# Group-norm statistics on ScalarE instead of VectorE, and more output buffers for the last image, in a fused attention and convolution kernel

## The chip, the cores and the metric

The kernel runs on one core of a Trainium2 chip. The core has a matrix engine (PE, TensorE; its weight loads are the rows PEld), a vector engine (DVE), an activation engine (ACT, ScalarE), a general engine (POOL, GpSimd) and a queue that only issues transfers (SP). ACT and SP both issue DMA transfers here. Every engine takes its instructions in order; an instruction that waits holds up all that stand behind it on the same engine. The metric is the device time of one execution in microseconds; smaller is better.

## The reference

Input x has the shape 16 x 56 x 56 x 384 (16 images of 3136 pixels, 384 channels), float32. Two layers are applied, each on a group-normalised copy of its input and added back to that input:

```python
def _gn(v, G=32, eps=1e-5):                 # per image and group of 12 channels
    g = v.reshape(B_, H_, W_, G, C_ // G)
    m = jnp.mean(g, axis=(1, 2, 4), keepdims=True)
    s = jnp.var(g, axis=(1, 2, 4), keepdims=True)
    return ((g - m) / jnp.sqrt(s + eps)).reshape(v.shape)
...
x = x + _L0_conv_ref(_gn(x), L0_conv_w_qkv, L0_conv_w_proj, L0_conv_b_proj)
x = x + _L1_conv_ref(_gn(x), L1_conv_w)
```

Layer 0 is a dilated attention: q, k and v are projections of the normalised x. The 384 channels are three groups of 128 with dilations 1, 2 and 3, each of four heads of 32 channels. Every pixel attends to its 3 x 3 dilated neighbours within its head: nine products of q and k, a softmax over the nine, and the weighted sum of nine v. The result is projected by w_proj and b_proj is added. Layer 1 is a 3 x 3 convolution, each channel by itself, with weights that are the signs of L1_conv_w.

The mean and the variance in `_gn` are what the change is about. They are over a whole image, so nothing of a layer can be normalised before all of that image's input to the layer is there.

## The kernel before

**Chunks and stages.** An image is cut into 7 chunks of 8 rows (448 pixels, PX), 112 chunks in all. On chip the channels are the partitions: a chunk is three tiles (j = 0, 1, 2) of 128 channels by 448 pixels. Three stages each run over all chunks, and work for different chunks is interleaved:

- *Stage A* (`plan_a`) loads x, turns it so that channels are partitions (PE, L412), copies the result from PSUM to `xa` on ACT (L424), takes its statistics on DVE (L425, `bn_stats`: count, mean and squared deviations of the even and of the odd elements, 6 numbers) and stores it to the DRAM scratch `xd`. Image 0 is kept in SBUF as `x_first` as well, and its store to `xd` is issued on ACT (L429); its 21 turns are all done ahead of any other work, because the first normalisation needs them all.
- *Stage B* (`plan_b`) normalises `xn` on ACT (L459), projects k and v (`pkv`) and q (`pq`) on PE (L463), copies k and v to SBUF on ACT (L473), forms the products `t` on DVE (L516), sums them over channels on PE (`ps`, L501), computes the softmax on ACT, DVE and POOL (`sT` L533, `ew`, `e`), spreads the weights over channels on PE (`pb_a`, L582), multiplies them with v on DVE (`w`, L589) and adds up on POOL (`w` L597, `y` L600 and L601). `out_project` multiplies y with w_proj on PE (`po`, L615), and DVE adds the bias and the residual (`xr`, L618) and takes the statistics of the new x (L621). The chunk is stored to the scratch `x1d`.
- *Stage C* (`plan_c`) loads from `x1d`, normalises on ACT (`z` L713, `zg` L756), convolves two channel groups on PE (`pc`, L727) and the third with ACT and POOL (`m`, L778 and L784), adds the residual (L734), turns the result back on PE (`pt_o`, L799), copies it to `osb` on ACT (L801) and stores it to the output (L804).

**Statistics.** At an image's last chunk `group_norm` combines them: `bn_aggr` on DVE over the 7 chunks of each j (L305, tile `ch`), sums over groups on PE (`pm`, `pb`, `pv`), the inverse root on DVE and POOL (`var`, L334 to L349), and the spread back to channels (`pp`, L354, to `mr`, L358, and for the convolution `mrz`, L372).

**The last image.** It is the tail: no later image covers it. Its stage C uses tiles that earlier stages have left (`z_last`, `xg_last`), DVE instead of POOL for the third channel group (L769), and issues its output on ACT. `osb` comes from pool `o_p` with two buffers: the third copy waits until the first one's transfer to the output has landed. The tiles `y`, in pool `y_p` with four buffers, are not used any more by then.

**What sets the order.** `at(when, order, piece)` gives each piece of work a time slot; a chunk takes 9 slots (STEP). Pieces are emitted by slot and, in a slot, by kind (SOFTMAX, SCORE, STATISTICS and so on). A scheduler then orders each engine's queue from this and adds the waits. Tiles of one tag share that tag's buffers in turn. In particular all PSUM tiles of tag `mt` (`pt_x`, `pkv`, `po`, `pc`, `pt_o` and those of the statistics) share three buffers, so PE's next such tile waits for an engine to have read the one three before it.

Of the kernel before, what the change touches and what calls it, by code (L numbers as in the profile page):

```python
# [8 lines left out]
F32 = mybir.dt.float32  # L9
BF16 = mybir.dt.bfloat16  # L10
I32 = mybir.dt.int32
AF = mybir.ActivationFunctionType
ALU = mybir.AluOpType
# [4 lines left out]
P = 128  # L18
HEADS = 4
HD = 32  # L20
NG = 3
# [3 lines left out]
SUB = 112  # L25
# [10 lines left out]
def dilated_attention_then_binary_conv(  # L36
# [28 lines left out]
    nc = tc.nc  # L65
    B, H, W, C = x.shape
    PX = ROWS * W
    NCH = H // ROWS
# [63 lines left out]
    bias = const.tile([P, NG], F32, name="bias")  # L132
# [12 lines left out]
    st_p = ctx.enter_context(tc.tile_pool(name="st_p", bufs=2))  # L145
# [5 lines left out]
    y_p = ctx.enter_context(tc.tile_pool(name="y_p", bufs=4))  # L151
# [5 lines left out]
    o_p = ctx.enter_context(tc.tile_pool(name="o_p", bufs=2))  # L157
# [137 lines left out]
    def group_norm(stats, done, for_convolution=False):  # L295
# [78 lines left out]

        return channels, mean, deviation, variance, invert, spread_out

    def chunk_of(dram, c):
        return dram.rearrange("(j p) n -> p j n", p=P)[:, :, c * PX : (c + 1) * PX]

# [2 lines left out]
    def at(when, order, piece):  # L382

        pieces.setdefault((when, order), []).append(piece)

    stats0, stats1 = {}, {}
# [4 lines left out]
    def plan_a(m, t0):  # L391

        b, c = divmod(m, NCH)
        had = {}

        def load():
            if c == 0:
                stats0[b] = st_p.tile([P, NG, NCH, 6], F32, tag="stats0", name="stats0")
                xd[b] = dr_p.tile([C, H * W], F32, tag="xd", name="xd")
            if b == 0 and c % 3:  # L400

                xin = z_p.tile([P, NQ * PX], F32, tag="z", name="xin_z")[:SUB, : NSUB * C]
                xin = xin.rearrange("p (s c) -> p s c", s=NSUB)
            else:
                xin = xin_p.tile([SUB, NSUB, C], F32, tag="xin", name="xin")
            had["xin"] = xin
            nc.sync.dma_start(xin, xf[b, c * PX : (c + 1) * PX, :].rearrange("(s p) c -> p s c", p=SUB))

        def turn(j):
            pt = ps_mt.tile([P, 512], F32, tag="mt", name="pt_x")  # L410
            for s in range(NSUB):
                nc.tensor.transpose(  # L412
                    pt[:, s * SUB : (s + 1) * SUB], had["xin"][:, s, j * P : (j + 1) * P], ident[:SUB, :SUB]
                )
            if b == 0:

                if j == 0:
                    pool, tag = ((xn_p, "xn"), (xn_p, "xn"), (xn_p, "xn"), (xr_p, "xr"), (t_p, "t"), (w_p, "w"),
                                 (w_p, "w"))[c]
                    first[c] = pool.tile([P, NG, PX], F32, tag=tag, name="x_first")  # L420
                xa = first[c][:, j]
            else:
                xa = xa_p.tile([P, PX], F32, tag="xa", name="xa")
            nc.scalar.copy(xa, pt[:, :PX])  # L424
            nc.vector.bn_stats(stats0[b][:, j, c, :], xa)  # L425
            if b:
                nc.sync.dma_start(xd[b][j * P : (j + 1) * P, c * PX : (c + 1) * PX], xa)
            elif j == NG - 1:
                nc.scalar.dma_start(chunk_of(xd[b], c), first[c])  # L429

        steps = {}

        def norm(k):
            if k == 0:
                steps["of"] = group_norm(stats0.pop(b), lambda mr: mr0.update({b: mr}))
            steps["of"][k]()

        at(t0 - 3 if b else FIRST + 2 * max(c - 2, 0), LOADS, load)
        for j in range(NG):
            at(t0 + 2 * j if b else FIRST + 2 * c + 1, STAGE_A, lambda j=j: turn(j))  # L440
        if c == NCH - 1:
            for k in range(6):
                at(t0 + 5 + STAT0_SLICE[k], STAT_ORDER[k], lambda k=k: norm(k))

    def plan_b(m, t0):

        b, c = divmod(m, NCH)
        had = {}

        def load_x():  # L450
            if m < 3:
                had["xn"] = first[m]
                return
            had["xn"] = xn = xn_p.tile([P, NG, PX], F32, tag="xn", name="xn")
            nc.sync.dma_start(xn, chunk_of(xd[b], c))
# [147 lines left out]
        def load_residual():  # L603
            had["xr"] = xr = xr_p.tile([P, NG, PX], F32, tag="xr", name="xr")
            nc.sync.dma_start(xr, chunk_of(xd[b], c))

        def out_project(j):

            if c == 0 and j == 0:
                stats1[b] = st_p.tile([P, NG, NCH, 6], F32, tag="stats1", name="stats1")  # L610
                x1d[b] = dr_p.tile([C, H * W], F32, tag="x1d", name="x1d")
            xr = had["xr"]
            po = ps_mt.tile([P, 512], F32, tag="mt", name="po")
            for g in range(NG):
                nc.tensor.matmul(  # L615
                    po[:, :PX], wprojT[:, g, j * P : (j + 1) * P], had[f"y{g}"], start=(g == 0), stop=(g == NG - 1)
                )
            nc.vector.scalar_tensor_tensor(  # L618
                xr[:, j, :], po[:, :PX], bias[:, j : j + 1], xr[:, j, :], op0=ALU.add, op1=ALU.add
            )  # L620
            nc.vector.bn_stats(stats1[b][:, j, c, :], xr[:, j, :])  # L621
            if j == NG - 1:
                nc.sync.dma_start(chunk_of(x1d[b], c), xr)

# [24 lines left out]
        for j in range(NG):  # L649
            at(t0 + 24 + j, PROJECT, lambda j=j: out_project(j))  # L650
# [4 lines left out]
    def plan_c(m, t0):  # L655

        b, c = divmod(m, NCH)
# [136 lines left out]
        def turn(s):  # L794
            pt = ps_mt.tile([P, 512], F32, tag="mt", name="pt_o")
            mid = had["xg"][:, 1 : ROWS + 1, :].rearrange("p r w -> p (r w)")
            for j in range(NG):
                src = mid if j == JG else had["x1"][:, j]
                nc.tensor.transpose(pt[:SUB, j * P : (j + 1) * P], src[:, s * SUB : (s + 1) * SUB], ident)  # L799
            osb = o_p.tile([SUB, C], F32, tag="osb", name="osb")  # L800
            nc.scalar.copy(osb, pt[:SUB, :C])  # L801

            queue = nc.sync if b < B - 1 else nc.scalar
            queue.dma_start(of[b, p0 + s * SUB : p0 + (s + 1) * SUB, :], osb)  # L804

        if b == B - 1:

            at(t0 - 12, LOADS, load_g)
            at(t0 - 3, LOADS, load_x)
            ahead = 8 if c else 1  # L810
            at(t0 - ahead, NORM, normalise_g)
            for j in range(JG):
                at(t0 - 12 + j, LOADS, lambda j=j: load(j))
                at(t0 - ahead + j, NORM, lambda j=j: normalise(j))
                at(t0 + 1 + j, CONVOLVE, lambda j=j: convolve(j))
            for ky in range(3):
                at(t0 + 1 + ky, CONVOLVE, lambda ky=ky: taps_last(ky))
            for s in range(NSUB):
                at(t0 + 12, STAGE_C, lambda s=s: turn(s))
            return  # L820
# [13 lines left out]
        for s in range(NSUB):  # L834
            at(t0 + 9 + s, STAGE_C, lambda s=s: turn(s))
# [51 lines left out]
```

## Time and profile before

| what | value |
|---|---|
| median of 8 runs | 5409.84 us (5406.19 to 5414.89) |
| the profiled execution, its own time | 5411.89 us |
| its span, first to last instruction | 5410.2 us |
| granted TensorE clock, mean | 0.981 |
| ACT L424, 128x448 copy of pt_x | 533 ns, x315 |
| ACT L459, normalise with two pointer operands, 128x448 | 751 ns, x327 |
| ACT L778, scale with one pointer operand, 128x448 | 658 ns, x945 |
| ACT L801, copy to osb, 112x384 | 481 ns, x448 |
| DVE L618, bias and residual | 678 ns, x336 |
| DVE L305, bn_aggr over 42 numbers | 336 ns, x96 |
| POOL L597, sum of weighted v, 128x1344 | 3051 ns, x672 |

A row of the profile's groups reads: line, engine, operation, output<-input, shapes, count | busy us, mean ns of one | idle us of the engine just ahead of them, and what ended that idle time. In a timeline a row is start, length, engine, line, operation and, in brackets, the idle time before it with its releaser. In the slices each digit is the busy share of a fortieth of the span in tenths. The list of waits gives the sum in us, how often, and the longest. The chain of waits is the work that ended last, followed back from the end.

### The profile page before, as it was taken

The page shows a single profiled execution, that of the slowest core. Times are in us where ns is not written, and L with a number is a line of the kernel's source. Part 1 is how long each engine was busy: PE and PEld are TensorE (multiplying, and loading weights), DVE is VectorE, ACT ScalarE, POOL GpSimd, SP SyncE. Part 2 cuts the span into 40 slices and gives each one's busy share as a digit, 9 for nine tenths or more (in the row PEclk, how much of TensorE's full clock was granted, in tenths as well). Part 3 has the DMA queues.
Part 4 walks back from the last instruction along what each step waited for, and adds up shares of the span by engine and source line. Part 5 has one row for each costly group of instructions (what it writes and reads, how often), then busy time and mean ns, then how long its engine had stood idle before and what let it go on. Part 6 is the DMA issues. An engine that isn't in the chain of part 4 may idle for free.

```text
span 5410.2 us, 77297 instructions
## 1 busy us (share of the span) xinstructions
PE 5202.6 (96%) x27669; PEld 2412.6 (45%) x27669; DVE 4153.8 (77%) x4209; ACT 2396.1 (44%) x4189; POOL 4215.2 (78%) x3049
## 2 busy tenths in 40 slices
PE   8999999999999999999999999999999999999965
PEld 4444444444444444444444444444444444444422
DVE  4887777878777787777878777787777877777753
ACT  3224444444444444444445444444444444444433
POOL 2677888878888887888878888888888888887880
PEclk9999999999999999999999999999999999999976
DMA  5444555655555555555655556555555555544443
GB/s 167 127 120 125 160 156 156 163 153 161 156 155 165 164 156 161 156 155 159 164 156 161 157 153 165 164 155 164 158 157 157 162 152 161 165 130 130 122 131 125
DMA packets 810799, 825.73 MB, mean 153 GB/s; under 512 B 359467, under 2 KB 800174, under 8 KB 810414
## 3 DMA queue, kind: packets, MB, share of 16 engines
q1 hardware_dynamic: 802430, 808.79, 53.9%
q10 hardware_dynamic: 7984, 12.00, 0.7%
q8 instruction: 219, 3.59, 0.3%
q14 instruction: 166, 1.36, 0.1%
HBM read 466.41 MB, written 231.21 MB: 129 GB/s over the span
## 4 chain that ended last, share of the span: by engine, by line
PE 72%; POOL 10%; DVE 6%; DMA 5%; ACT 4%; issue 2%; SPq 1%; POOLq 0%; ACTq 0%; DVEq 0%
PE pkv L463 22%; PE pq L463 12%; PE po L615 10%; PE ps L501 9%; PE pc L727 8%; PE pb_a L582 4%; POOL w L597 3%; POOL m L784 3%; DVE t L516 2%; PE pt_o L799 2%; PE pt_x L412 2%; DVE w L589 2%; ACT m L778 2%; DMA xg<-x1d 1%; POOL m L789 1%
## 5 line engine op out<-in xcount | busy, mean ns | idle before, releaser
L597 POOL TENSOR_TENSOR w<-w 128x1344 f32<-128x1344 f32 x672 | 2050.0, 3051 | 452.6 <-DVE w L589 388.7
L589 DVE TENSOR_TENSOR w<-pb_a,v 128x1344 f32<-128x1344 f32 x1008 | 1560.1, 1548 | 268.1 <-PE pb_a L582 177.9
L516 DVE TENSOR_TENSOR t<-pq,k 128x1344 f32<-128x1344 f32 x1008 | 1536.6, 1551 | 236.9 <-PE pq L463 235.9
L463 PE MATMUL pkv<-xn,wqkvT 128*128 128x448 f32 x3924 | 1568.4, 548 | 9.0 <-ACT xa L424 4.7
L463 PEld LDWEIGHTS pkv<-xn,wqkvT 128*128 128x128 f32 x3924 | 717.9, 190 | 671.7 <-issue 631.4
L615 PE MATMUL po<-y,wprojT 128*128 128x448 f32 x2016 | 838.4, 552 | 33.7 <-ACT k L473 15.8
L784 POOL TENSOR_TENSOR m<-m 128x1344 f32<-128x1344 f32 x210 | 644.7, 3070 | 282.5 <-ACT m L778 282.4
L463 PE MATMUL pq<-xn,wqkvT 128*128 128x448 f32 x1962 | 830.7, 557 | 0.0
L713 ACT ACTIVATE z<-z,mrz 96x448 f32<-96x448 f32 x840 | 578.2, 751 | 359.7 <-DMA z<-x1d 339.6
L501 PE MATMUL ps<-t,sel 128*32 128x448 f32 x6048 | 663.7, 548 | 27.8 <-DVE t L516 27.1
L778 ACT ACTIVATE m<-zg,ktap 128x448 f32<-128x448 f32 x945 | 555.5, 658 | 275.4 <-POOL m L784 268.3
L615 PEld LDWEIGHTS po<-y,wprojT 128*128 128x128 f32 x2016 | 377.6, 192 | 390.5 <-issue 342.3
L727 PE MATMUL pc<-z,kdiag 96*32 96x440 f32 (+1 forms) x5040 | 514.6, 541 | 6.6 <-POOL z L715 4.6
L463 PEld LDWEIGHTS pq<-xn,wqkvT 128*128 128x128 f32 x1962 | 343.9, 189 | 316.9 <-issue 316.9
L618 DVE SCALAR_TENSOR_TENSOR xr<-po,bias,xr 128x448 f32<-128x448 f32 x336 | 227.7, 678 | 230.6 <-PE po L615 226.9
L734 DVE TENSOR_TENSOR x<-pc,x 128x448 f32<-128x448 f32 x224 | 139.4, 623 | 344.3 <-PE pc L727 333.4
L582 PE MATMUL pb_a<-aT,spread 24*128 24x448 bf16 x3024 | 368.8, 359 | 32.3 <-DVE w L589 25.4
L601 POOL TENSOR_TENSOR y<-y,w 128x448 f32<-128x448 f32 x336 | 381.6, 1136 | 22.6
L600 POOL TENSOR_TENSOR y<-w 128x448 f32<-128x448 f32 x336 | 382.4, 1138 | 14.7
L473 ACT COPY v<-pkv 128x448 f32<-128x448 f32 x336 | 178.4, 531 | 480.7 <-PE pkv L463 472.4
L473 ACT COPY k<-pkv 128x448 f32<-128x448 f32 x336 | 178.2, 530 | 375.7 <-PE pkv L463 375.7
L501 PEld LDWEIGHTS ps<-t,sel 128*32 128x32 f32 x6048 | 170.2, 109 | 368.5 <-issue 252.3
(131 smaller groups left out, 4395.7 us busy)
## 6 DMA issues: line engine op xcount, KB each, us to landing
z<-x1d SPq DMA_DIRECT2D x570, 224.0 KB
xr<-xd SPq DMA_DIRECT2D x112, 672.0 KB
x1d<-xr SPq DMA_DIRECT2D x112, 672.0 KB
xn<-xd SPq DMA_DIRECT2D x109, 672.0 KB
xin<-in_x_dram SPq DMA_DIRECT2D x108, 672.0 KB
xd<-xa SPq DMA_DIRECT2D x315, 224.0 KB
out_dram<-osb SPq DMA_DIRECT2D x420, 168.0 KB
x<-x1d SPq DMA_DIRECT2D x112, 448.0 KB
```

The lines of the kernel that those rows point to most:

```text
L463: nc.tensor.matmul(dst[:, :PX], wqkvT[:, cc, o0 : o0 + P], had["xn"][:, cc, :], start=(cc == 0), stop=(cc == NG - 1))
L501: return nc.tensor.matmul(had["ps"][32 * j : 32 * j + 32, :PX], sel[:, s0 : s0 + 32], tk, start=(issued[j] == 1), stop=(issued[j] == len(r ...
L516: nc.vector.tensor_tensor(t.rearrange("p k (r w) -> p k r w", w=W), q3, k3, ALU.mult)
L582: return nc.tensor.matmul(pb[:, kx, :PX].rearrange("p (s n) -> p s n", s=NSUB), spread[rows_of, v % 2, :], had["a"][rows_of, :, v // 8, :] ...
L589: nc.vector.tensor_tensor(w.rearrange("p k (r w) -> p k r w", w=W), pb[:, :, :PX].rearrange("p k (r w) -> p k r w", w=W), three(kv[1][g][m ...
L597: nc.gpsimd.tensor_tensor(w0, w0, w, ALU.add)
L600: nc.gpsimd.tensor_tensor(y, w0[:, 0], w0[:, 1], ALU.add)
L615: nc.tensor.matmul(po[:, :PX], wprojT[:, g, j * P : (j + 1) * P], had[f"y{g}"], start=(g == 0), stop=(g == NG - 1))
L713: nc.scalar.activation(z, z, AF.Identity, bias=mrz[:, j, q, 0:1], scale=mrz[:, j, q, 1:2])
L727: return nc.tensor.matmul(pcr[q * HD : (q + 1) * HD, :, lo:hi], kdiag[:, kx, j * NQ + q, :], rows(set_of(j, q))[:, :, lo + kx - 1 : hi + k ...
L778: nc.scalar.activation(rows(t[:, kx]), zp[:, ky : ky + ROWS, kx : kx + W], AF.Copy, scale=ktap[:, o : o + 1])
L784: nc.gpsimd.tensor_tensor(had["m"], had["m"], t, ALU.add)
```

## The change

Two parts are changed.

*Statistics.* Where DVE had one `bn_stats` per tile there are now: a sum over the 448 pixels that the instruction writing the tile gives as a second output (`accum_out`: ACT's copy in `turn`, DVE's addition in `out_project`), a `mul` on ACT of 128x1 that makes the mean of it, and a `Square` on ACT over the whole tile, with the mean as bias, whose summed output is the squared deviation (its elementwise output goes to a tile `squares` of one buffer that nobody reads). An entry is now count, mean and squared deviation, 3 numbers, with the count set on POOL once per tile of statistics. `total`, the sum, has two buffers, shared by both layers. `bn_aggr` is as before, over 21 numbers.

*Output.* For the last image, `osb` is taken from the four buffers of `y` instead of the two of `osb`.

```diff
+    def new_statistics(name):
+
+        stats = st_p.tile([P, NG, NCH, 3], F32, tag=name, name=name)
+        nc.gpsimd.memset(stats[:, :, :, 0:1], float(PX))
+        return stats
+
+    def statistics(entry, xa, total):
+        nc.scalar.mul(entry[:, 1:2], total, 1.0 / PX)
+        squares = st_p.tile([P, PX], BF16, tag="squares", name="squares", bufs=1)
+        nc.scalar.activation(
+            squares, xa, AF.Square, bias=entry[:, 1:2], scale=-1.0, accum_out=entry[:, 2:3]
+        )
...
-            nc.scalar.copy(xa, pt[:, :PX])
-            nc.vector.bn_stats(stats0[b][:, j, c, :], xa)
+            total = st_p.tile([P, 1], F32, tag="total", name="total")
+            nc.scalar.activation(xa, pt[:, :PX], AF.Copy, accum_out=total)
+            statistics(stats0[b][:, j, c, :], xa, total)
...
+            total = st_p.tile([P, 1], F32, tag="total", name="total")
             nc.vector.scalar_tensor_tensor(
-                xr[:, j, :], po[:, :PX], bias[:, j : j + 1], xr[:, j, :], op0=ALU.add, op1=ALU.add
+                xr[:, j, :], po[:, :PX], bias[:, j : j + 1], xr[:, j, :], op0=ALU.add, op1=ALU.add, accum_out=total
             )
-            nc.vector.bn_stats(stats1[b][:, j, c, :], xr[:, j, :])
+            statistics(stats1[b][:, j, c, :], xr[:, j, :], total)
...
-            osb = o_p.tile([SUB, C], F32, tag="osb", name="osb")
+            if b < B - 1:
+                osb = o_p.tile([SUB, C], F32, tag="osb", name="osb")
+            else:
+                osb = y_p.tile([P, PX], F32, tag="y", name="osb_last")[:SUB, :C]
             nc.scalar.copy(osb, pt[:SUB, :C])
```

In the two places where a tile of statistics is made, `new_statistics` takes the place of a tile of 6 numbers per entry.

More of the change, by code (lines that the diff above doesn't have):

```diff
@@ L397, in load @@
             if c == 0:
-                stats0[b] = st_p.tile([P, NG, NCH, 6], F32, tag="stats0", name="stats0")
+                stats0[b] = new_statistics("stats0")
                 xd[b] = dr_p.tile([C, H * W], F32, tag="xd", name="xd")
@@ L609, in out_project @@
             if c == 0 and j == 0:
-                stats1[b] = st_p.tile([P, NG, NCH, 6], F32, tag="stats1", name="stats1")
+                stats1[b] = new_statistics("stats1")
                 x1d[b] = dr_p.tile([C, H * W], F32, tag="x1d", name="x1d")
```

## The prediction

> **What bounds the kernel now.** First the page's busy shares and slices.
>
> ```profile
> PE 5202.6 (96%) x27669; PEld 2412.6 (45%) x27669; DVE 4153.8 (77%) x4209; ACT 2396.1 (44%) x4189; POOL 4215.2 (78%) x3049
> PE   8999999999999999999999999999999999999965
> ```
>
> PE is full except in the first and the last two slices. The table by windows says how full (columns: window, its length, busy time and count for PE, PEld, DVE, ACT, POOL, granted clock, DMA share, GB/s).
>
> ```profile
> 1000.00:2000.00 1000.00, 987.14 (x5303) 459.79 (x5305) 789.39 (x793) 467.69 (x820) 820.32 (x566) 0.99 0.57 158
> 5250.00:5300.00 50.00, 34.20 (x246) 14.90 (x246) 19.89 (x43) 18.81 (x30) 6.94 (x24) 0.65 0.41 131
> ```
>
> In the middle PE idles 13 us in 1000, and its timeline inside an image runs from matmul to matmul without a gap. A freer VectorE can return at most what PE waits for there. The list of waits of PE between 100 and 5150 us (us in total, times, longest):
>
> ```profile
> PE ps L501 <- DVE t L516: 24.3, 35, 1.5
> PE po L615 <- ACT k L473: 15.8, 13, 2.7
> PE pb_a L582 <- DVE w L589: 11.0, 18, 1.0
> PE pv L331 <- POOL dev L325: 9.6, 11, 0.9
> ```
>
> So 35 us name DVE. DVE's timeline ahead of one such wait (PE idle 1.46 us until 1162.70) shows who was late: POOL, by 1.96 us, not bn_stats.
>
> ```profile
> 1158.79 1.56 DVE L589 TENSOR_TENSOR w<-pb_a,v 128x1344 f32<-128x1344 f32 x1 [1.96 <-POOL w L597]
> 1160.27 0.92 DVE L547 TENSOR_REDUCE sm<-ew 112x48 f32<-112x432 f32 x1
> 1161.09 1.56 DVE L516 TENSOR_TENSOR t<-pq,k 128x1344 f32<-128x1344 f32 x1
> ```
>
> What moves the end is therefore the two ends. At the start, PE's projections wait for image 0's statistics; at the tail, ACT's copies to osb wait for output transfers. Both chains are below.
>
> **What the Trainium skill says.** "ScalarE: Activation LUTs", section "What ACT_TABLE_LOAD costs": an ACTIVATE with immediates takes 186 ns + 0.833 ns per element, each pointer operand adds 93 ns, neighbours overlap by about 93 ns. The trace agrees: one pointer at 448 elements gives 652, measured 658 (m, L778); two give 745, measured 751 (xn, L459); three copies back to back took 1.40 us, a pitch of 0.435 for rows of 0.533. The page says that an ACTIVATE can give an accumulator output, but no price. "VectorE: DVE Perf Modes", section "Two Vector instructions with no wait between them": on VectorE such an op is two instructions, the second reading the accumulator; no row of before shows one. [...] The built program accordingly has mul wait for the sum and Square for mul, so these cannot overlap fully.
>
> **The change part by part.**
>
> ```profile
> L621 DVE BATCH_NORM_STATS2 stats<-xr 128x6 f32<-128x448 f32 x336 | 208.4, 620 | 3.8
> L425 DVE BATCH_NORM_STATS2 stats<-xa 128x6 f32<-128x448 f32 x315 | 191.3, 608 | 63.7 <-ACT xa L424 63.5
> ```
>
> *DVE loses* 208.4 + 191.3 + 11.9 (image 0) = 412 us, 3.7 us per chunk (46 us: the same wait of PE recurs after one image, 322.9 us, of 7 chunks), and bn_aggr reads 21 numbers instead of 42 (all 96 cost 31.9 us now). The sum added to L618 costs 0 to 0.13 us (DVE's smallest rows), at most 44 us. All beside PE. Of the 35 us I credit 3, since POOL sets the waits; bounds 0 and 35.
>
> *ACT gains* 672 mul of 128x1 (0.187 by the skill: 126 us), 672 Square with a bias pointer (0.658 as L778: 442 us) and 1008 sums. A sum's unknown cost lies between 0 (read in the shadow of the next instruction) and 0.19 (one more instruction of fixed cost); below nothing is excluded, since the copy itself stays. I take 0.1: 101 us. ACT goes from 2396 to 3065 us, 57%, or from 21.4 to 27.4 us per chunk. Three new couplings: mul waits for DVE's L618; L618 waits, through the two buffers of total, for an earlier mul; and bn_aggr on DVE waits for Square, with w and t queued behind it. Inside an image each has cover. Between k's copy (ends 681.5) and z (685.42, waiting 3.91 us for DMA) ACT is idle, which takes two mul and one Square. The other Square delays sT from 687.25 to about 688.1, and PE wants it at 690.52. If that cover went, it would cost up to 0.85 us per chunk. At the two statistics per image, bn_aggr can wait for a Square that stands behind a z waiting for DMA: I put 0.2 us for each of 15 images, +3 us, bounds 0 and 30.
>
> *32 memsets on POOL* (0.15 us, as L752) are 5 us in 1195 us of POOL idle time: nothing; uncovered, 5 us.
>
> *The start.* ACT's timeline:
>
> ```profile
> 8.13 0.53 ACT L424 COPY x_first<-pt_x 128x448 f32<-128x448 f32 x1 [3.54 <-PE pt_x L412]
> 16.64 1.40 ACT L424 COPY x_first<-pt_x 128x448 f32<-128x448 f32 x3 [3.17 <-DMA small<-in_L_conv_b_proj_dram]
> 36.14 1.04 ACT L424 COPY x_first<-pt_x 128x448 f32<-128x448 f32 x2
> ```
>
> The last bn_aggr ends at 41.56 us; ACT's copies are done at 37.2. Now all 21 statistics run on ACT. One chunk is 3 copies, 3 mul, 3 Square and the issue of xd: 1.45 (pitch 0.435, one overlap lost to a wait) + 0.53 + 1.78 (pitch 0.56, the last 0.66) + 0.41 = 4.2 us, 4.7 with sums at 0.1, 5.4 with 0.19. In the built order chunk 0's last Square and all of chunk 1 stand behind the xd issue, which waits for a small transfer as at 16.23 (now the next one of the queue, so about 17). From there: 0.7 + 6 x 4.7 + 9 weight copies (1.3 for three) 3.9 = 49.8, and 0.3 for bn_aggr: 50.1 against 41.56, +8.5. Next image's mul and Square between the first normalisations add 0.5. **+9**, bounds +5 (sums free) and +13. Nothing covers it: from 60 us on PE is full, so its work shifts whole.
>
> *The tail.* The chain of waits (start, us, what):
>
> ```profile
> 5366.44 5.87 DMA out_dram<-osb
> 5372.39 0.49 ACT osb L801
> ...
> 5378.14 3.26 DMA out_dram<-osb
> ...
> 5383.37 3.61 DMA out_dram<-osb
> ...
> 5396.19 3.85 DMA out_dram<-osb
> ...
> 5401.55 2.14 DMA out_dram<-osb
> ...
> 5404.27 2.09 DMA out_dram<-osb
> ```
>
> With four buffers for two: before 5372.39 ACT idles 1.44 us, of which 1.4 goes. The later waits let convolutions start at about 5387.5, not 5390.38, so 1.5 more goes (2.9 in all). The last eight copies now start at 5395.7 and end at 5406.9 in pairs that wait for transfers. With four they wait once: four copies and issues to about 5398.5, one wait to 5400.1, four more to 5402.8, 4.1 earlier. **-7**. From 5302 to 5353 SP issues loads of z_last without pause, 2.3 us each, so nothing is gained there. Bounds: -2 (only part of the last pairs, since an issue on ACT can still wait for another transfer) and -15 (of the 20.8 us above). Last statistics: Square in place of bn_stats, mul and two semaphores, +1 (0 to 2).
>
> Sum: -3 + 3 + 9 - 7 + 1 = +3 on this execution's 5411.9 us (span 5410.2 and 1.7 around it), which is 2.1 above the median 5409.8. Predicted against the median: **5413 us**.
>
> **Rivals.** Two tenths of a per cent, 10.8 us, is about what a measurement tells from no change.
> *ACT holds DVE, slower.* bn_aggr waits for a Square which waits behind z's DMA (3.91 us idle above) or m's POOL (2.7 us), and w and t, so PE, wait behind it. At 1.5 us per image's statistics, 15 images give +22 for the 3 above: 5432. It passes +0.2% from about 0.7 us per image. For: PE already waits for ACT k at 13 boundaries. Against: Square stands early in ACT's built order, and DVE has 3.7 us more room per chunk.
> *DVE's relief pays, faster.* If two thirds of the 35 us go, since w, t and POOL's w sums all come earlier, -23 for -3: 5393; with the better tail 5385. For: 53 waits name DVE. Against: POOL stands before them.
> *The start is hidden.* DMA is busy at 9 tenths until 40 us; if arrival of x paces ACT, +1 for +9: 5405.
>
> **How the numbers follow.** Forecast 0.40 (own range 5405 to 5420), ACT holds DVE 0.30, relief pays 0.17, hidden start 0.13. Forecast and hidden start are within 0.2%: 0.53; slower 0.30; faster 0.17. The range cuts a third of the slow case and half of the fast one: 5392 to 5438.
>
> **What would show it.** PE's first projection (52.13 now) at about 61; ACT near 3065 us with Square near 0.66; PE's waits for DVE t and w still near 35 us; no copy of the last image waiting over 2 us for out_dram except once at the end. Wrong if PE idles over 20 us per 1000 in the middle (then bn_aggr shows a wait for Square), or if the waits for t and w vanish.

## The result, and the profile after

| kernel | median us | against before |
|---|---|---|
| before | 5409.1 (5402.0 to 5415.0, 32 runs) | |
| changed | 5424.5 (5421.3 to 5432.6, 12 runs) | ratio 1.0030, 95% interval 1.0022 to 1.0037 |

The change costs 15.4 us, 0.3%: slower, by more than the two tenths of a per cent below which the prediction counts a difference as none. The profiled execution of the changed kernel took 5433.9 us (span 5431.8), 9.4 above its median, so the differences of the two profiles (21.6 us of span) are read for where, and the medians for how much.

The changed kernel's busy shares and PE's slices:

```profile
PE 5222.1 (96%) x27669; PEld 2418.2 (45%) x27669; DVE 3797.5 (70%) x3873; ACT 2986.6 (55%) x6541; POOL 4210.4 (78%) x3081
PE   7999999999999999999999999999999999999975
```

VectorE gave up 356 us and ScalarE took on 590. PE, with the same 27669 matmuls, is busy 19.5 us longer. In the middle PE idles 14.5 us in 1000 (12.9 before); the table by windows, columns as in the prediction:

```profile
1000.00:2000.00 1000.00, 985.46 (x5294) 457.73 (x5295) 716.06 (x723) 580.54 (x1268) 814.90 (x569) 0.99 0.58 159
```

PE's waits between 100 and 5150 us have nearly the same sum as before (78 us for 77), but other names:

```profile
PE pkv L477 <- ACT xa L438: 23.8, 14, 1.9
PE po L629 <- ACT k L487: 19.6, 13, 2.9
PE pt_x L425 <- PE pkv L477: 11.4, 15, 0.8
PE pb_a L596 <- DVE w L603: 7.2, 4, 4.3
PE pv L331 <- POOL dev L325: 6.5, 8, 0.9
PE ps L515 <- DVE t L530: 0.7, 1, 0.7
```

The waits for t and w fell from 35.3 to 7.9 us. In their place pkv waits for the copy to xa, 14 times, about once an image, where before it waited once (4.7 us), and pt_x waits for pkv.

The start of an image's normalisation, DVE's write of mr (L358), is a good milestone, since it comes twice an image. The lag of the changed kernel behind before at these, in the two profiles: first one (51.12 before) +8.2; the 31st (4989.58) +31.8; the last one, with which the last image's stage C begins (5271.75), +25.7; end +21.6. So the start costs 8.2, the middle 23.6, and 10.2 come back in the last image: 6.1 ahead of its stage C, 4.1 in it.

**Where the middle loses.** At 1884.78 us PE has waited 1.90 us for xa. ACT's timeline in the changed kernel around it:

```profile
1876.00 0.63 ACT L572 CAST e<-ew 112x512 bf16<-112x512 f32 x1
1883.57 0.62 ACT L577 CAST e<-rest 112x512 bf16<-112x512 f32 x1 [6.94 <-POOL rest L573]
1884.09 0.54 ACT L438 ACTIVATE xa<-pt_x 128x448 f32<-128x448 f32 x1
```

POOL's timeline there, with rest as the last:

```profile
1876.95 3.03 POOL L611 TENSOR_TENSOR w<-w 128x1344 f32<-128x1344 f32 x1
...
1880.09 1.12 POOL L614 TENSOR_TENSOR y<-w 128x448 f32<-128x448 f32 x1
1881.29 1.14 POOL L615 TENSOR_TENSOR y<-y,w 128x448 f32<-128x448 f32 x1
1882.38 1.15 POOL L573 TENSOR_TENSOR rest<-ew,e 112x512 f32<-112x512 f32 x1
```

And PE's, which has nothing to do between the two rows:

```profile
1882.16 0.72 PE L354 MATMUL pp<-pair,gselT 32*128 32x2 f32 x6
1884.78 6.47 PE L477 MATMUL pkv<-xn,wqkvT 128*128 128x448 f32 x12 [1.90 <-ACT xa L438]
```

Read it backwards. pkv needs a PSUM buffer that the copy to xa empties. (e holds the softmax weights cut into bf16 parts, and rest is what a first part leaves over: ACT writes the first part, POOL subtracts it, ACT writes the second.) The copy stands on ACT behind e (L577), which waits 6.94 us for POOL's rest. rest could have started at 1876.63, when e (L572) ended; but in POOL's queue a sum of w and both sums of y stand ahead of it, 5.4 us. Before, at the same point of an image, the queue was the other way round, as POOL's timeline of the kernel before shows, and pkv did not wait:

```profile
1865.04 1.15 POOL L559 TENSOR_TENSOR rest<-ew,e 112x512 f32<-112x512 f32 x1
1866.15 3.03 POOL L597 TENSOR_TENSOR w<-w 128x1344 f32<-128x1344 f32 x1
1869.15 1.15 POOL L564 TENSOR_TENSOR e<-rest,e 112x512 bf16<-112x512 f32 x1
```

No line of the diff touches rest, w or y. The change took instructions from one queue and put others in another, and the scheduler, which orders each queue anew, put rest last at the change of images. ACT itself is not short of time there: it idles 6.94 us.

**The second half of the price.** The x12 group of pkv above takes 6.47 us; the same group after 1.55 us of waiting, at 907.56, took 4.78, which is its usual length. A row of the table by windows shows what differs: PE was granted 0.66 of its clock.

```profile
1885.00:1890.00 5.00, 5.00 (x10) 2.26 (x10) 2.37 (x2) 3.22 (x8) 3.54 (x3) 0.66 0.67 141
```

Of the long groups (six or twelve matmuls of pkv, pq or po) between 100 and 5150 us, 14 ran more than 0.5 us over their usual length in the changed kernel, 25.6 us in all; before it was 4, with 7.8 us. Twelve of the 14 came right after a wait of 1.1 to 1.9 us and ran 1.7 to 1.8 us over. So a wait of under 2 us can cost PE as much again afterwards, and most of the 19.5 us of extra busy time is of this kind.

### The profile page after: what moved, and what is told of

Its sections match the earlier page's. It is cut to its first block, busy times and chain, and to the rows that moved or that the text cites. A ratio compares the mean times of both kernels' runs of the same rounds, so it can differ in the third digit from the quotient of the medians.

```text
span 5431.8 us, 79669 instructions
## 1 busy us (share of the span) xinstructions
PE 5222.1 (96%) x27669; PEld 2418.2 (45%) x27669; DVE 3797.5 (70%) x3873; ACT 2986.6 (55%) x6541; POOL 4210.4 (78%) x3081
## 5 line engine op out<-in xcount | busy, mean ns | idle before, releaser
L633 DVE SCALAR_TENSOR_TENSOR xr<-po,bias,xr 128x448 f32<-128x448 f32 x336 | 228.7, 681 | 289.9 <-PE po L629 154.6
L438 ACT ACTIVATE xa<-pt_x 128x448 f32<-128x448 f32 x315 | 171.4, 544 | 321.5 <-PE pt_x L425 321.2
```

## The experiments

Each time is read against the kernel before, run beside it on the same chip: 5412.9 us for the runs up to "POOL's order put back"; for the later ones 5411.9 (base, rest held back, first pin) and 5414.2 us (changed kernel, two pins).

### Output part alone

```diff
-            osb = o_p.tile([SUB, C], F32, tag="osb", name="osb")
+            if b < B - 1:
+                osb = o_p.tile([SUB, C], F32, tag="osb", name="osb")
+            else:
+                osb = y_p.tile([P, PX], F32, tag="y", name="osb_last")[:SUB, :C]
```

> Only the output part of the change: the kernel before, with the last image's osb in the four buffers of y. Theory (the tail gain is real and independent of the statistics): about 8 us faster than before, 5401, between -5 and -11; in the changed kernel's profile 10 us of the lag that stands at the last image's normalisation are gone at the end. Rival (the loads of z_last set the tail, and the two buffers waited beside them): within 2 us of before.

Measured: 5403.9, 9.0 below before (ratio 0.9985, interval 0.9976 to 0.9994). The end of its chain of waits:

```profile
5386.59 0.49 ACT osb_last L804
...
5388.13 2.32 DMA out_dram<-osb_last
...
5390.98 0.48 ACT osb_last L804
```

The last eight copies now wait twice for a transfer, 0.55 and 0.62 us, where they waited up to 3.57 us before. From the first of them to the end of the last issue it is 5.6 us instead of 11.6. From the last mr to the end it is 129.2 us instead of 138.4. The gain is real and needs nothing of the statistics.

### Statistics of stage A alone, and of out_project alone

From the changed kernel, with osb back in its own two buffers; either the first pair of hunks is undone (out_project alone) or the second (stage A alone):

```diff
-            nc.scalar.activation(xa, pt[:, :PX], AF.Copy, accum_out=total)
-            statistics(stats0[b][:, j, c, :], xa, total)
+            nc.scalar.copy(xa, pt[:, :PX])
+            nc.vector.bn_stats(stats0[b][:, j, c, :], xa)
...
-                xr[:, j, :], po[:, :PX], bias[:, j : j + 1], xr[:, j, :], op0=ALU.add, op1=ALU.add, accum_out=total
+                xr[:, j, :], po[:, :PX], bias[:, j : j + 1], xr[:, j, :], op0=ALU.add, op1=ALU.add
-            statistics(stats1[b][:, j, c, :], xr[:, j, :], total)
+            nc.vector.bn_stats(stats1[b][:, j, c, :], xr[:, j, :])
```

> Only the statistics of stage A on ScalarE; out_project keeps bn_stats, osb its two buffers. Built, POOL's order at the change of images is that of the kernel before (rest ahead of the w sum). Theory (POOL's order makes the new waits): the start costs 9, no wait of pkv for xa appears at the change of images, and half of VectorE's relief brings some 10: within 6 us of before, 5403 to 5415. Rival (ScalarE's load makes the copies of xa late): half of the new work is here, and all of it in the engine's queue ahead of or behind xa: start 9 and some 10 to 15 in the middle, about 5430, with waits of pkv for xa.

> Only the statistics of out_project on ScalarE; stage A keeps bn_stats, osb its two buffers. Built, POOL's order at the change of images is that of the changed kernel (the w sum and both y ahead of rest). Theory (POOL's order): 14 stalls of pkv for xa of 1.5 to 1.9 us and matmuls at a lower clock after them, together some +39, against a relief of 15 to 25 and no cost at the start: +14 to +24, 5423 to 5433. Rival (ScalarE's load): half of the load, no start, so less than the whole change costs: 5409 to 5416.

Measured: stage A alone 5505.0, 92 above before (ratio 1.0170, 1.0156 to 1.0184): both expectations missed. out_project alone 5415.2, within the error of before (1.0005, 0.9997 to 1.0013): the rival's number, not the theory's.

Stage A alone shows the same chain of waits in another place. The order at the change of images was as in the kernel before; but at another chunk of each image, xg and a sum of w had moved ahead of rest. ACT's timeline there:

```profile
1797.61 0.62 ACT L572 CAST e<-ew 112x512 bf16<-112x512 f32 x1
1807.78 0.62 ACT L577 CAST e<-rest 112x512 bf16<-112x512 f32 x1 [9.55 <-POOL rest L573]
1808.30 0.54 ACT L438 ACTIVATE xa<-pt_x 128x448 f32<-128x448 f32 x1
```

POOL's, with xg and w ahead of rest:

```profile
1802.49 1.15 POOL L806 TENSOR_TENSOR xg<-m,xg 128x448 f32<-128x448 f32 x1
1803.60 3.03 POOL L611 TENSOR_TENSOR w<-w 128x1344 f32<-128x1344 f32 x1
1806.60 1.15 POOL L573 TENSOR_TENSOR rest<-ew,e 112x512 f32<-112x512 f32 x1
```

And PE's, 4.19 us idle:

```profile
1808.98 6.93 PE L477 MATMUL pkv<-xn,wqkvT 128*128 128x448 f32 x12 [4.19 <-ACT xa L438]
```

In the kernel before rest stood ahead of xg at this chunk, and e waited 5.42 us there without pkv waiting behind it. The wait of pkv for xa is 59.8 us in 15 times. out_project alone has the changed kernel's order at the change of images, and there 14 waits for xa, 20.3 us; but its waits for t fell from 24.3 to 4.5 and those of po for k from 15.8 to 2.8, while those for w rose from 11.0 to 16.0. The theory had the wait right and the sum wrong; a new wait of pt_x, 20.4 us in 14 times, has no releaser in the profile, and the balance was not taken apart further. Their first projections stand at 61.07 (stage A alone) and 52.89 us (out_project alone).

### POOL's order put back

The changed kernel, with the order of two POOL instructions pinned (no wait is added; both are on POOL), and the piece with rest emitted one slot earlier to that end:

```diff
-            nc.gpsimd.tensor_tensor(rest.rearrange(EIGHTS, k=8), e8, term[0], ALU.subtract)
+            last_rest[m] = nc.gpsimd.tensor_tensor(rest.rearrange(EIGHTS, k=8), e8, term[0], ALU.subtract)
...
-            nc.gpsimd.tensor_tensor(w0, w0, w, ALU.add)
+            added = nc.gpsimd.tensor_tensor(w0, w0, w, ALU.add)
+            if i == 5 and m + 1 in last_rest:
+                tc.add_manual_dep(
+                    added.ins, last_rest[m + 1].ins.name,
+                    mybir.DependencyInfo(mybir.DependencyClass.NoSync, mybir.DependencyReason.DATA), reason="order",
+                )
...
-        at(t0 + 11, SOFTMAX, softmax_3)
+        at(t0 + 10, SOFTMAX, softmax_3)
```

> The changed kernel with one pin in POOL's order: rest is issued ahead of the w sum that overtook it at the change of images, as in the kernel before. The other engines' orders stay as in the changed kernel but for a few lines at the last image. Theory (POOL's order): the 14 waits of pkv for xa (23.8 us) go, and with them most of the 19.5 us that PE is longer busy: some 39 us less than the changed kernel, about 5386 (5378 to 5396), faster than before. Rival (ScalarE's load): the waits of pkv for xa stay, 5420 to 5428. Third (the stall moves to the next late engine): xa's waits go, others of the same sum come, about 5415 to 5424.

In the two traces PE, DVE, ACT and SP start their instructions in the order of the changed kernel but for some 16 of them; on POOL, rest, the e that follows from it and a memset have moved, and two sums of w.

Measured: 5394.0, 18.9 below before (ratio 0.9963, 0.9950 to 0.9975), some 34 below the changed kernel when each is set against its own before. Its longest waits of PE:

```profile
PE po L635 <- ACT k L488: 18.3, 13, 2.0
PE pt_x L426 <- PE pkv L478: 10.6, 13, 0.9
PE pb_a L597 <- DVE w L604: 10.3, 5, 4.4
...
PE ps L516 <- DVE t L531: 3.7, 4, 1.6
```

ACT's timeline at the same place of the same image:

```profile
1865.55 0.62 ACT L578 CAST e<-rest 112x512 bf16<-112x512 f32 x1 [1.29 <-POOL rest L574]
1869.36 0.54 ACT L439 ACTIVATE xa<-pt_x 128x448 f32<-128x448 f32 x1 [3.19 <-PE pt_x L426]
```

e waits 1.29 us for rest instead of 6.94, the copy to xa now waits for PE, and pkv's wait for xa is gone from the list. PE's waits between 100 and 5150 us come to 53.5 us in all, for 77 before. PE is busy 5205.8 us, 16.3 less than in the changed kernel. All of ScalarE's new work is still there (2990.7 us). So in the middle neither Square nor the sums made the loss. This version beats both kernels.

### The order alone, in the kernel before

These and the runs below have a base of their own: they leave out the transposition of e into aT. Its DMA (L569 before) is two plain copies of the same bytes, so the weights that are spread are other data, and the output is not the reference's. They are read against that base.

```diff
-            nc.sync.dma_start(
-                aT.rearrange("p s u n -> p (s u) n"), e3.rearrange("p s u k -> p (s u k)"), transpose=True
-            )
+            flat, e_flat = aT.rearrange("p s u n -> p (s u n)"), e3.rearrange("p s u k -> p (s u k)")
+            half = NSUB * NPAD // 8 * SUB
+            nc.sync.dma_start(flat[:SUB], e_flat[:, :half])
+            nc.sync.dma_start(flat[SUB:], e_flat[: P - SUB, :half])
```

> A base for the runs beside it: the kernel before, but the DMA that turns e into aT is replaced by two plain copies of the same bytes, so that the weights spread over the channels are other data; all orders on the engines stay but for a few neighbours. Both theories expect the time of before within 10 us (5400 to 5422), since aT lands long ahead of its use: PE waits for it only 4 times now.

Measured: 5426.3, 14.3 above before (1.0029, 1.0017 to 1.0041), more than expected: pv's waits for dev grew from 9.6 to 17.1 us. More than a few neighbours moved, too: on ACT some 390 of 4228 instructions, mostly z, start in another order than before, and on POOL a sum of w in 15 images.

With rest held behind the second sum of y at the change of images; the edit names nothing else:

```diff
+            subtract = nc.gpsimd.tensor_tensor(rest.rearrange(EIGHTS, k=8), e8, term[0], ALU.subtract)
+            if m % NCH == 4 and (m - 1, 1) in last_y:
+                tc.add_manual_dep(
+                    subtract.ins, last_y[m - 1, 1].ins.name,
+                    mybir.DependencyInfo(mybir.DependencyClass.NoSync, mybir.DependencyReason.DATA), reason="order",
+                )
```

> The base with plain copies for aT, nothing of the change in it, but with rest issued on POOL behind the w sum and both y at the change of images, as in the changed kernel. Theory (the order alone makes the wait of pkv for xa, whoever takes the statistics): some 15 waits of 1.5 to 2.5 us and matmuls at a lower clock after them, +30 to +55 us on the base. Rival (ScalarE's new work makes the wait): within 5 us of the base, since ScalarE has none of it.

Measured: 5473.0, 61.1 above before, so 46.7 above the base. The wait has the changed kernel's name and count, with bn_stats still on VectorE:

```profile
PE pkv L464 <- ACT xa L425: 28.9, 14, 4.7
```

The base has this wait once (4.7 us), and PE's busy time grew from 5204.1 to 5224.2 us. PE and DVE keep the base's order to the last instruction. But the scheduler moved more than rest: at the chunk after, in 13 images, two sums of w on POOL and four instructions on ACT stand elsewhere. Of the 32 us by which PE's waits grew between 100 and 5150 us, 24.2 are for xa. So order makes this wait, whoever takes the statistics; the 46.7 us are not all rest's.

### The changed kernel and its repairs on that base

> The changed kernel whole, with the plain copies for aT of the base (which stood at 5426 where before stood at 5412). POOL's order at the change of images is that of the changed kernel. Theory: as with the real transfers, 15 above its base, so about 5441 (5434 to 5452), with waits of pkv for xa near 24 us. Rival (the stall hangs on when aT lands): no waits of pkv for xa, and at or below the base.

> Plain copies for aT as in the base; the changed kernel with both repairs: POOL's order pinned (rest ahead of the w sum) and image 0's statistics of stage A with bn_stats. Theory (the two costs add): the pinned one was 19 below before, and the start gives 8 more: 27 below the base (24 to 31). Rival (one hides the other): 17 to 21 below, as with the pin alone.

> The changed kernel with plain copies for aT and two pins on POOL: rest ahead of the w sum, and the first sum of m (ky = 1) ahead of the chunk's first w sum. In the run with the first pin alone, POOL's w sum stood ahead of that m sum at one chunk of each image, ScalarE's next m waited for it, and pv waited up to 3.0 us for dev, 41 us in all. The order is now that of the run that was 19 below before. Theory (POOL's order, at both places): pv's waits fall under 18 us and the time is about 19 below the base, 5407 (5398 to 5416). Rival (the relief is worth little with these transfers): within 6 us of the base.

> As the run with two pins, and image 0's statistics of stage A with bn_stats. The first projection stands at 53.4 us instead of 61 to 62 where that was done. Theory (what is late at the start is late at the end): 8 us below the run with two pins (5 to 10), about 5399. Rival (it is caught up on the way): within 3 us of it.

The second pin, and image 0:

```diff
+                if ky == 1 and c and m + 8 in first_w:
+                    tc.add_manual_dep(
+                        first_w[m + 8].ins, added.ins.name,
+                        mybir.DependencyInfo(mybir.DependencyClass.NoSync, mybir.DependencyReason.DATA), reason="order",
+                    )
...
+            if b == 0:
+                nc.scalar.copy(xa, pt[:, :PX])
+                nc.vector.bn_stats(stats0[b][:, j, c, :], xa)
```

| kernel | us | over its before | over the base |
|---|---|---|---|
| base | 5426.3 | +14.3 | |
| changed | 5462.2 | +48.0 | +33.7 |
| first pin, image 0 with bn_stats | 5421.7 | +9.7 | -4.6 |
| two pins | 5411.2 | -3.0 | -17.3 |
| two pins, image 0 with bn_stats | 5403.4 | -10.8 | -25.1 |

The column over the base is the one before it less the base's own 14.3. The two runs with two pins came as the theory expected. The whole change costs 34 on this base and not 15, and the first pin brings less than expected, both for one reason. This is the longest of PE's waits for POOL in the changed kernel on this base:

```profile
PE pv L331 <- POOL dev L325: 41.2, 14, 3.0
```

The same with the first pin and image 0:

```profile
PE pv L331 <- POOL dev L325: 41.3, 14, 3.0
```

And with two pins:

```profile
PE pv L331 <- POOL dev L325: 16.5, 12, 1.6
```

With the other transfers POOL's queue had come out differently at one more chunk of each image: a sum of w ahead of the first sum of m, on which ACT's next m and then dev hang. The second pin takes that away. The changed kernel and the first pin missed both of their expected numbers. Both pins together are worth 51 us here, with the arithmetic and the load of every engine unchanged. Image 0 gives 7.8 us, as expected (8): the first mr moves from 60.67 to 51.43 us, and what is late there is late at the end. On the real transfers image 0 was not measured, neither alone nor with the pin.

### Stage A alone, pinned

> Plain copies for aT as in the base, and only the statistics of stage A on ScalarE, as in the run that was 92 above before, with the pin that issues rest ahead of the w sum on POOL. There xg and a w sum had overtaken rest at another chunk of each image, and ScalarE stood 9.55 us in front of e, with xa behind it. Theory (POOL's order made those 15 waits of up to 4.2 us): they go, and what is left is the start's 9 less some relief of VectorE: within 8 us of the base. Rival (the sums and Squares between xa's copies on ScalarE make them): at least 40 above the base.

> Only the statistics of stage A on ScalarE, plain copies for aT, and both pins on POOL. With the first pin alone it stood 90 above the base, pv waiting 41 us for dev, t and w later than before. Theory (POOL's order at the second place made the rest): pv's waits fall under 18 us and the time comes within 20 us of the base, 9 of it the start. Rival (with bn_stats still in out_project, ScalarE's sums in stage A cost PE time by themselves): over 50 above the base.

Measured: one pin 5516.4, 90 above the base; two pins 5490.8, 62 above it. The theory's numbers are missed both times; they are the rival's. The waits for xa did fall, from 59.8 to 17.6 us, but pv's wait for dev (41.3 us, 14 times) had come; the second pin took that to 17.0. What then stays: xg is still ahead of rest on POOL, with e waiting 6.57 us and xa behind it (17.7 us); and the waits for t and w are 64 us against 35 in the base:

```profile
PE ps L516 <- DVE t L531: 32.7, 33, 1.9
PE pb_a L598 <- DVE w L605: 31.2, 30, 3.1
PE pkv L478 <- ACT xa L439: 17.7, 14, 1.9
```

Why they grew was not isolated. So it isn't shown that order explains all of this case.

## Why the prediction was right and wrong

The median, 5424.5, lies in the range (5392 to 5438). The likeliest case, no change at 5413, was not what happened: the time is slower by 0.28%, a case with a chance of 0.30.

- *DVE's relief, -3 credited.* This step failed: the term was too small, and the reading behind it did not hold. From one wait, in which POOL was late by 1.96 us, the prediction concluded that "POOL sets the waits". PE's waits for t and w, 35.3 us, fell to 7.9, and to 14.0 in the pinned kernel. That kernel gains 19 us in the middle: 8.6 behind before at the first mr (59.74), it is 10.5 ahead at the 31st (4979.04). This is about the size of the "relief pays" rival (-23). At the very place that the prediction read, POOL is later still in the changed kernel, and yet PE does not wait for t (only 0.79 us for pt_x just before):

```profile
1170.32 1.56 DVE L603 TENSOR_TENSOR w<-pb_a,v 128x1344 f32<-128x1344 f32 x1 [2.57 <-POOL w L611]
1172.31 1.55 DVE L530 TENSOR_TENSOR t<-pq,k 128x1344 f32<-128x1344 f32 x1
1173.77 0.93 DVE L561 TENSOR_REDUCE sm<-ew 112x48 f32<-112x432 f32 x1
```

  Here, and in 94 of the 112 chunks, t now stands ahead of the row sum sm on DVE; before it stood behind. No line of the diff names this either. Every run that has out_project's statistics on ScalarE has the new order, and PE waits at most 4.5 us for t in it; every other run has the old one and 14.4 us or more, stage A alone included, though it too relieves VectorE. No run changes this order by itself, so it stays open how much of the 19 us comes from a lighter VectorE and how much from the order of its queue. The prediction's own sign of error, these waits vanishing, is what the trace shows.
- *The coupling, +3 at 0.2 us per image.* The mechanism named does occur: bn_aggr waited for Square between 100 and 5150 us:

```profile
DVE ch L305 <- ACT squares L386: 64.7, 36, 4.1
```

  It costs little: the pinned kernel has 61.5 us of it and is 18.9 us faster than before. The same goes for the rival "ACT holds DVE", whose 5432 is near the result for another reason. What was missing is a term for the order of POOL's queue: the prediction went by the built order of ACT and took POOL's as it was, where rest had moved. On the real transfers this order is worth some 34 us; with the second place of that kind on the other base, 51.
- *The start, +9.* Right. The first projection is at 61.60 us (61 predicted), the lag at the first mr is 8.2, and undoing it for image 0 gave 7.8. ACT stood 7.29 us behind the issue of xd, and two copies with sums stand 0.52 us apart, 0.085 more than the 0.435 without (0.1 assumed), as ACT's timeline of the changed kernel shows:

```profile
11.66 0.19 ACT L384 ACTIVATE stats<-total 128x1 f32<-128x1 f32 x1
18.72 0.38 ACTq L443 DMA_DIRECT2D xd<-x_first  x1
19.15 0.67 ACT L386 ACTIVATE squares<-x_first,stats 128x448 bf16<-128x448 f32 x1 [7.29 <-DMA small<-in_L_conv_w_dram]
19.81 0.52 ACT L438 ACTIVATE x_first<-pt_x 128x448 f32<-128x448 f32 x1
20.33 0.53 ACT L438 ACTIVATE x_first<-pt_x 128x448 f32<-128x448 f32 x1
```

- *The tail, -7.* Right in kind: 9.0 alone. In the changed kernel's profile only 4.1 come back within the last image's stage C (134.4 us from the last mr to the end). In its chain of waits the transfer to the output is down to one short row, and loads of z_last stand ahead of the last convolution:

```profile
5394.66 7.87 DMA z_last<-x1d
...
5413.32 9.27 PE pc L742 x48
...
5423.99 2.44 DMA out_dram<-osb_last
```

- *Last statistics, +1.* The last two bn_aggr wait 0.59 and 1.15 us for Square. As expected, and too small to test.
- *ACT's load, 3065 us.* Measured 2986.6. Square takes 0.666 and 0.670 (0.658 taken), mul 0.205 (0.187), and overlaps hide more than was reckoned. Nothing hangs on it.

The sum by what was found, in the profiles: start +8, middle +24, last image -10, together +22 (at the medians +15). The pinned kernel has +9, -19 and -8, together -18. So the order at the change of images costs some 43 us of the middle (34 at the medians), and what is left of the change gains 19 there. That the median fell in the range is luck in this respect: a gain of 19 that was put at 3, and a loss of 34 or more that no term held, partly made up for each other.

## What to carry to other kernels

Where a scheduler orders the queues, compare the built order of every engine before and after an edit, also of those that the edit does not name; here one instruction that moved behind three others on POOL turned a gain of 19 us into a loss of 15. One wait, read at one place, does not say what a whole sum of waits hangs on: here the instruction waited for got another place in its own queue. Measure such a change again with the order pinned before judging what the moved work costs.

## What the runs showed of the hardware

- *Short waits of PE are paid twice, sometimes.* In the changed kernel PE waited 1 to 2 us ahead of 25 long groups between 100 and 5150 us. Twelve of them then ran 1.7 to 1.8 us over their usual length and 13 did not: after 1.13 us (1855.18) six matmuls of po took 4.22 instead of 2.42 us, after 1.91 us (2212.27) twelve of pkv took their usual 4.78. The Trainium skill, "TensorE: Matmul & The Clock Gate", section "What's actually happening", gives two clocks, half and full, and a free-running window of 3413 ns. By that, as an estimate, half speed for one window loses 1.7 us, which agrees with these twelve. The page puts the drop after an idle window of about 3.4 us; here it comes after waits of a third of that, and not after each.
- *An accumulator output is a second instruction.* ACT shows a read of 187 to 197 ns per sum that overlaps its neighbours (pitch about 0.09 us). On DVE it is 83 ns after L633, which itself went from 678 to 681 ns.
